# TensorE's order in the last attention: a written table of every score and transposed score in place of a string of letters

## The chip, the cores and the metric

The kernel runs on one core of a Trainium2 chip. The metric is the device time of one execution in microseconds (us), as the median of several runs; a profiled execution of the same program gives the trace. The engines are TensorE (PE; its weight loads are listed as PEld), VectorE (DVE), ScalarE (ACT), GpSimd (POOL) and SyncE (SP, which issues transfers).

## The reference, cut to what matters

A stream x of shape 2 x 512 x 512 (batch, position, width; float32) passes through eight blocks, each of the form x = x + block(layernorm(x)): four attentions and four feed-forward blocks. The change touches the last attention alone, a causal multi-head attention with 32 heads of 16:

```
qkv = hidden_states @ qkv_w + qkv_b
q, k, v = split into 32 heads of 16; rope on q and k
scores = einsum('bqhd,bkhd->bhqk', q, k) / 4, causal mask
probs  = softmax(scores)
ctx    = einsum('bhqk,bkhd->bqhd', probs, v)
return ctx @ out_w + out_b
```

## The kernel before, in words

The 32 heads are worked off as 8 quartets of four heads. A head's 16 features lie in a group of 32 partitions, so that the four heads of a quartet lie in the four row groups of TensorE, and matmuls of different heads g = 0 to 3 can run beside each other. Positions are cut into four tiles of 128. Everything is done once per batch, by `core(b, causal)`; a flag computed from the weights chooses the causal branch, which is the one that the trace shows.

For each quartet u there are these steps:

- `score(u, qt, g)` (L1572): the scores of query tile qt against keys 0 to 128 (qt + 1), so 128, 256, 384 or 512 columns, into a bank of PSUM. VectorE adds the mask and takes the row maximum (L1585), one column of the tile `nm[u % 2]`. 16 of them.
- `maxima(u)` (L1596): four transposes bring the maxima of the quartet into rows, and VectorE adds them to the queries (`qm`, L1601), so that the maximum comes off in the next product. It needs all 16 scores of the quartet.
- `transposed(u, kc, g)` (L1604): the transposed scores of key tile kc, 512, 384, 256 or 128 columns. ScalarE takes the exponential (L1621) into the tile `pt` of that key tile; after the fourth head GpSimd sets the upper triangle of the diagonal block to zero (L1625). 16 of them.
- `values(u)` (L1630): 16 matmuls over the four key tiles, in the order kc = 0 to 3, into one bank (L1636), copied to `raw` by ScalarE (L1644). Each key tile needs its mask of L1625.
- `divide(u)` (L1646): four transposes of `raw` (L1650), then a reciprocal and a product on VectorE (L1653, L1654).

Every step takes one of the eight banks of PSUM in rotation through `turn()`, so the step that stands eight places earlier must have been read (by VectorE for a score, by ScalarE for a transposed score) before a step can write.

TensorE's order is written by hand: within `tc.manual_schedule` (L1661) the steps stand on its queue as the Python code issues them. The other engines take the work in that order too. `run_ordered` (L389) issues eight scores in front, and then for each quartet walks the string `order`: S takes the next score from an iterator that goes through all quartets (tile by tile, heads in the order 0, 2, 1, 3), T the next transposed score of quartet u (key tile by key tile, heads 1, 3, 0, 2), M stands for the maxima of quartet u + 1, and | for the division of quartet u - 1. Values of quartet u follow at the end of the string. So scores run half a quartet to one and a half ahead of the transposed scores.

## Time and profile before

| what | us |
|---|---|
| median of 3 runs (lowest to highest) | 2110.02 (2104.93 to 2113.53) |
| the profiled execution | 2103.46 |
| its span, first to last instruction | 2101.4 |
| first score to first values, batch 0 (1785.11 to 1804.60) | 19.49 |
| five full periods from the first values to the sixth (1804.60 to 1855.21) | 50.61 |
| from the sixth values to the last division (1855.21 to 1876.40) | 21.19 |

The profiled execution has a time of its own, 2.1 us over its span. Times within the trace count from the span's start. A row of the windows view gives a stretch, its length, and each engine's busy time in it with the number of instructions; PEclk is the granted TensorE clock. A row of the timeline gives start, duration, engine, line, operation, output and inputs, and in brackets how long the engine had been idle and what released it. The last attention takes two stretches of the trace, one for each batch, from about 1785 and from about 1935 us.

### The profile page before, as it was taken

The page shows a single profiled execution, that of the slowest core. Times are in us where ns is not written, and L with a number is a line of the kernel's source. Part 1 is how long each engine was busy: PE and PEld are TensorE (multiplying, and loading weights), DVE is VectorE, ACT ScalarE, POOL GpSimd, SP SyncE. Part 2 cuts the span into 40 slices and gives each one's busy share as a digit, 9 for nine tenths or more (in the row PEclk, how much of TensorE's full clock was granted, in tenths as well). Part 3 has the DMA queues.
Part 4 walks back from the last instruction along what each step waited for, and adds up shares of the span by engine and source line. Part 5 has one row for each costly group of instructions (what it writes and reads, how often), then busy time and mean ns, then how long its engine had stood idle before and what let it go on. Part 6 is the DMA issues. An engine that isn't in the chain of part 4 may idle for free. (4 is left out here: it accounts for less than half of the span.)

```text
span 2101.4 us, 40138 instructions
## 1 busy us (share of the span) xinstructions
PE 2031.9 (97%) x15560; PEld 1147.1 (55%) x15560; DVE 1351.0 (64%) x3575; ACT 745.4 (35%) x2072; POOL 970.4 (46%) x1239
## 2 busy tenths in 40 slices
PE   9999999999999999999999989999999999999998
PEld 5444435666666566666665544545454454654654
DVE  7678766756566566666664557666666784855845
ACT  3555632222222222222222145444544411441531
POOL 1101016776555557566653246555555555115220
PEclk9999999999999999999999999999999999999999
DMA  3001012222222222222220321010101003002001
GB/s 100 16 21 41 1 66 76 72 76 71 91 71 71 91 71 76 71 91 76 73 77 26 117 61 54 22 51 25 50 22 52 2 6 70 2 2 41 2 2 40
DMA packets 70221, 107.43 MB, mean 51 GB/s; under 512 B 13699, under 2 KB 50691, under 8 KB 63237
## 3 DMA queue, kind: packets, MB, share of 16 engines
q1 hardware_dynamic: 69380, 103.71, 15.6%
q8 instruction: 126, 2.06, 0.4%
q10 hardware_dynamic: 640, 1.05, 0.3%
q14 instruction: 75, 0.61, 0.1%
HBM read 80.61 MB, written 2.10 MB: 39 GB/s over the span
## 5 line engine op out<-in xcount | busy, mean ns | idle before, releaser
L263 ACT ACTIVATE room<-room,nmax 128x128 f32<-128x128 f32 (+3 forms) x384 | 212.3, 555 | 484.2 <-DVE nmax L253 482.7
L274 POOL TENSOR_SCALAR room<-room,invs 128x128 f32<-128x128 f32 (+3 forms) x384 | 198.0, 537 | 142.1 <-DVE invs L271 142.1
L314 PE MATMUL sc<-turned,vals 32*128 32x128 f32 (+7 forms) x1034 | 186.2, 411 | 1.3 <-DVE turned L287 1.3
L314 PE MATMUL pj<-turned,vals 32*128 32x384 f32 (+7 forms) x708 | 184.9, 422 | 0.0
L210 POOL TENSOR_TENSOR rstd<-ve,mhalf 128x1 f32<-128x1 f32 x80 | 45.9, 577 | 246.0 <-DVE ve L208 240.2
L314 PE MATMUL tp<-turned,vals 32*128 32x256 f32 (+7 forms) x770 | 147.1, 420 | 2.5 <-DMA vals<-v 2.1
L242 PE MATMUL sc<-kT,q 128*32 128x256 f32 (+4 forms) x1528 | 134.0, 384 | 6.8 <-DVE invs L271 4.1
L287 DVE STREAM_TRANSPOSE turned<-room 128x1152 f32<-128x1152 f32 x80 | 109.1, 1363 | 42.4 <-POOL room L274 39.9
L314 PEld LDWEIGHTS sc<-turned,vals 32*128 32x128 f32 (+1 forms) x1034 | 119.3, 166 | 14.3 <-issue 4.2
L943 POOL TENSOR_TENSOR q<-q,cosq 128x512 f32<-128x512 f32 x60 | 89.5, 1491 | 59.9 <-DVE t L940 59.9
L162 PE MATMUL sc<-w,room 128*128 128x512 f32 (+1 forms) x256 | 112.1, 582 | 0.0
L314 PEld LDWEIGHTS pj<-turned,vals 32*128 32x128 f32 (+1 forms) x708 | 104.0, 169 | 4.0 <-issue 1.6
L314 PEld LDWEIGHTS tp<-turned,vals 32*128 32x128 f32 (+1 forms) x770 | 97.6, 169 | 10.8 <-issue 4.9
L162 PE MATMUL sc<-w,ctxT 128*128 128x512 f32 x224 | 101.5, 596 | 0.0
L218 DVE TENSOR_TENSOR x<-sc,x 128x512 f32<-128x512 f32 x79 | 54.2, 686 | 73.0 <-PE sc L162 70.3
L242 PE MATMUL tp<-kT,q 128*32 128x512 f32 (+4 forms) x984 | 91.7, 407 | 4.5 <-DVE invs L271 3.8
L274 POOL TENSOR_SCALAR probs<-probs,invs 128x128 f32<-128x128 f32 (+3 forms) x128 | 65.8, 535 | 65.0 <-DVE invs L271 61.2
L263 ACT ACTIVATE probs<-probs,nmax 128x128 f32<-128x128 f32 (+3 forms) x128 | 71.1, 556 | 65.5 <-DVE nmax L253 64.3
L253 DVE CUSTOM_DVE_ANT_0 room<-sc,mask 128x256 f32<-128x256 f32 (+3 forms) x149 | 70.7, 474 | 35.6 <-PE sc L242 34.1
L242 PE MATMUL pj<-kT,q 128*32 128x288 f32 (+3 forms) x968 | 89.6, 404 | 2.9 <-POOL q L1211 1.9
L944 POOL TENSOR_TENSOR q<-q,t 128x512 f32<-128x512 f32 x64 | 88.0, 1374 | 6.5 <-DVE q L943 2.5
L1208 POOL TENSOR_TENSOR t<-t,sinq 128x512 f32<-128x512 f32 x32 | 40.8, 1276 | 106.4 <-DVE invs L271 100.6
(621 smaller groups left out, 6232.9 us busy)
## 6 DMA issues: line engine op xcount, KB each, us to landing
w<-in_b_wq SPq DMA_DIRECT2D x16, 1024.0 KB, 4.9
w<-in_b_wo SPq DMA_DIRECT2D x16, 1024.0 KB, 5.2
vals<-v SPq DMA_DIRECT2D x256, 64.0 KB, 2.0
w<-in_m_wo SPq DMA_DIRECT2D x8, 1024.0 KB, 7.2
w<-in_b_wk SPq DMA_DIRECT2D x16, 256.0 KB, 2.5
w<-in_b_wupv SPq DMA_DIRECT2D x16, 256.0 KB, 2.5
w<-in_f_w SPq DMA_DIRECT2D x4, 1024.0 KB, 6.0
w<-in_m_wqn SPq DMA_DIRECT2D x8, 384.0 KB, 3.1
```

The source lines that it names most:

```text
L162: last = self.nc.tensor.matmul(out, lhsT, rhs, start=(i == 0), stop=(i == len(pairs) - 1))
L210: self.nc.gpsimd.tensor_tensor(r, ve, self.mhalf, ALU.pow)
L218: self.latest = self.nc.vector.tensor_tensor(self.x[t], ps, self.x[t], ALU.add).ins
L242: nc.tensor.matmul(ps[32 * i : 32 * i + 32, a - lo : b - lo], q[:, at : at + 32], keys[:, a:b], start=True, stop=True,)
L253: nc.vector.tensor_tensor_reduce(out=row, in0=ps[:, :kv], in1=self.mask_back[:, :kv] if qt % 2 else self.mask[:, S - kv :], op0=ALU.add, o ...
L263: nc.scalar.activation(row, row, AF.Exp, bias=nmax, scale=-1.0, accum_out=total[:, qt : qt + 1])
L274: self.nc.gpsimd.tensor_scalar(row, row, inv[:, qt : qt + 1], 1.0, ALU.mult, ALU.mult)
L287: self.nc.vector.transpose(out[:, :last], probs[:, :last])
L314: self.nc.tensor.matmul(out[:, :, :n], values(i, j), rhs, start=(j == blocks[0]), stop=(j == stop[i]),)
L943: mul.tensor_tensor(q, q, tables["cosq"], ALU.mult)
L944: nc.gpsimd.tensor_tensor(q, q, t2, ALU.add)
L1208: nc.gpsimd.tensor_tensor(t2, t2, sinq, ALU.mult)
```

## The change

`run_ordered` is replaced by `in_order`, and the string by a table. An entry such as `S21+1` is one step: the kind, the tile, the head, and how many quartets ahead of the round p it works (S score, T transposed, V values, D division, M maxima). `in_order` walks the table once for each p from -3 to 10 and leaves out entries whose quartet does not exist. So each round issues 16 scores, of quartets p + 1, p + 2 and p + 3, 14 transposed scores of quartet p and two of quartet p - 1, the values of p - 1, the division of p - 2 and the maxima of p + 1. The values stand fourth in the table, right behind the two last transposed scores of their quartet (T12-1, T31-1); division and maxima stand side by side. The steps themselves are not changed.

```diff
-    def run_ordered(n, lead, order, score, maxima, transposed, values, after):
-        scores = iter([(u, j, g) for u in range(n) for j in range(NT) for g in (0, 2, 1, 3)])
-        for i in range(lead):
-            score(*next(scores))
-        for u in range(-1, n):
-            left = [(j, g) for j in range(NT) for g in (1, 3, 0, 2)] if u >= 0 else []
-            for step in order:
...
-            if u >= 0:
-                values(u)
-        after(n - 1)
+    def in_order(n, order, do):
+        steps = [(s[0], int(s[1]), int(s[2]), int(s[3:])) if s != "|" else s for s in order.split()]
+        for p in range(-3, n + 3):
+            for step in steps:
+                if step == "|":
+                    if p > -3:
+                        do(p, step)
+                elif 0 <= p + step[3] < n:
+                    do(p + step[3], *step[:3])
...
-                order = "STTSTSSTSTTSTSTSTTTTS|TTSTMTSSSSSS"
-                k.run_ordered(8, 8, order, score, maxima, transposed, values, divide)
+                order = (
+                    "S21+1 T12-1 T31-1 V00-1 S01+2 T23+0 T32+0 S10+2 T11+0 S22+2 T03+0 S00+2 "
+                    "T02+0 T01+0 T10+0 S13+1 S12+2 T33+0 D00-2 M00+1 S02+3 T20+0 T21+0 S03+2 "
+                    "T22+0 S20+3 T13+0 S11+3 T30+0 S23+3 T00+0 S31+3 S32+2 S30+3 S33+3 "
+                )
+
+                def do(u, kind, *at):
+                    steps = dict(S=score, T=transposed)
+                    if kind in steps:
+                        steps[kind](u, *at)
+                    elif kind != "|":
+                        dict(M=maxima, V=values, D=divide)[kind](u)
+
+                k.in_order(8, order, do)
```

More of the change, by code (lines that the diff above doesn't have):

```diff
@@ L388, in run_ordered @@
     @staticmethod
-    def run_ordered(n, lead, order, score, maxima, transposed, values, after):
-        scores = iter([(u, j, g) for u in range(n) for j in range(NT) for g in (0, 2, 1, 3)])
-        for i in range(lead):
-            score(*next(scores))
-        for u in range(-1, n):
-            left = [(j, g) for j in range(NT) for g in (1, 3, 0, 2)] if u >= 0 else []
-            for step in order:
-                if step == "S":
-                    at = next(scores, None)
-                    if at:
-                        score(*at)
-                elif step == "T" and left:
-                    transposed(u, *left.pop(0))
-                elif step == "M" and u + 1 < n:
-                    maxima(u + 1)
-                elif step == "|" and u > 0:
-                    after(u - 1)
-            if u >= 0:
-                values(u)
-        after(n - 1)
+    def in_order(n, order, do):
[7 more added lines that the diff above has]
+                    do(p + step[3], *step[:3])
 def attn_latent_small(k, a):
```

## The prediction

> **What bounds the kernel now.** I read the page first, then the windows of this stage, then who the score reductions waited for, then the timeline of one quartet. The page:

> ```profile
> span 2101.4 us, 40138 instructions
> PE 2031.9 (97%) x15560; PEld 1147.1 (55%) x15560; DVE 1351.0 (64%) x3575; ACT 745.4 (35%) x2072; POOL 970.4 (46%) x1239
> ```

> TensorE (PE) is busy nearly everywhere, so whatever it is kept from in this stage lengthens the run. But four row groups of 32 work beside each other here, and "busy" means that at least one does. The windows tell more: ramp, full quartets and tail of the first batch, then one full quartet (from one block of values to the next).

> ```profile
> core 0: us, PE busy (x) PEld busy (x) DVE busy (x) ACT busy (x) POOL busy (x), PEclk, DMA share, GB/s
> 1785.11:1804.60 19.49, 16.75 (x121) 12.06 (x121) 17.70 (x74) 5.81 (x16) 2.05 (x4) 0.82 0.01 2
> 1804.60:1855.21 50.61, 50.54 (x520) 30.77 (x521) 42.71 (x178) 31.03 (x85) 12.60 (x21) 1.00 0.01 2
> 1855.21:1876.40 21.19, 21.10 (x200) 12.42 (x201) 9.41 (x34) 12.74 (x35) 5.72 (x9) 1.00 0.01 2
> 1834.97:1845.09 10.12, 10.11 (x104) 6.14 (x105) 8.54 (x38) 6.18 (x17) 2.54 (x5) 1.00 0.00 0
> ```

> A full quartet takes 10.12 us and holds 8.54 us of VectorE (DVE) work. The gap stands in one place:

> ```profile
> 1836.72 0.14 DVE L1585 DVE_READ_ACCUMULATOR2_ANT nm<- 128x1 f32 x1
> 1838.32 0.57 DVE L1585 CUSTOM_DVE_ANT_0 sc<-sc,mask 128x384 f32<-128x384 f32 x1 [1.45 <-PE pj L1575]
> 1834.97 1.06 PE L1636 MATMUL tp<-room,vs 128*32 128x512 f32 x8
> 1835.83 0.85 PE L1636 MATMUL tp<-pt,vs 128*32 128x384 f32 x8
> 1836.47 0.64 PE L1636 MATMUL tp<-room,vs 128*32 128x256 f32 x8
> 1836.90 0.43 PE L1636 MATMUL tp<-pt,vs 128*32 128x128 f32 x8
> 1837.26 0.58 PE L1575 MATMUL sc<-ks,qs 32*128 32x384 f32 x1
> ```

> For 2.29 us (1834.97 to 1837.26) TensorE does the values. VectorE has 1.9 us of scores in hand, then waits 1.45 us for the first new one; the rest of the period it runs without a gap, and TensorE waits for banks that it holds. So VectorE plus one hole sets 10.12 us. The streaming rate is read here too: eight passes over four column groups took 0.86 us for 512 columns, so 0.43 us a pass, 0.32, 0.21 and 0.11 for 384, 256 and 128. Each score and transposed score is two passes on its row group.

> The path of the transposed scores:

> ```profile
> 1829.81 0.62 ACT L1621 ACTIVATE room<-tp 128x512 f32<-128x512 f32 x1
> 1830.56 0.64 POOL L1625 TENSOR_SCALAR_AFFINE_SELECT room<-room 128x512 f32<-128x512 f32 x1 [5.09 <-ACT room L1621]
> 1873.13 0.64 POOL L1625 TENSOR_SCALAR_AFFINE_SELECT room<-room 128x512 f32<-128x512 f32 x1 [0.47 <-ACT room L1621]
> 1873.81 0.64 POOL L1625 TENSOR_SCALAR_AFFINE_SELECT pt<-pt 128x512 f32<-128x512 f32 x1
> ```

> The fourth exponential of a key tile ends at 1830.43, GpSimd's mask starts 0.13 us later and takes 0.64. The values of that tile need it. Before, key tile 0 is masked 4.4 us ahead of its values (1830.56 against 1834.97), so this costs nothing.

> **The change, part by part.** No instruction is added or removed: per batch 128 scores, 128 transposed, 8 maxima, values and divisions. ScalarE's, VectorE's and GpSimd's orders follow TensorE's; SP has nothing to do in the stage. The sums below are for one batch; there are two.

> *The ramp.* A reduction starts 0.245, 0.385, 0.515 or 0.65 us after the one before (1834.94, 1835.19, 1835.58; 1838.80 to 1839.31; 1791.26 to 1791.91), so 16 of them take 7.18 us. Before, the first maxima need 16 reductions: they start at 1793.49, 7.4 after the first reduction (1786.06). In the table 27 reductions stand in front (all of quartet 0, eleven of quartet 1): 12.2 us, so +5.0. From there to the second maxima VectorE has the maxima's wait 0.5, the sum 0.61, nine scores of 4.5 and six of 2.3: 8.0 us. It bounds this stretch, since the transposed scores stand behind banks that it must free. Then 4.6 us (next paragraph) to the first values: 12.7, against 1793.49 to 1804.60 = 11.1. The first values come 5.0 + 1.6 = 6.6 us later. ScalarE and TensorE idle meanwhile, and what is ahead must be given back later.

> *A full quartet.* I lay the table out on the four row groups from the first matmul after the maxima (0). T00 gets its bank from T21, whose exponential ends at 1.45; it starts at 1.5, its two passes 0.86 and the drain 0.16 end at 2.5, the exponential runs 2.6 to 3.2, the mask 3.33 to 3.97, and values may start at 4.05. Matmuls alone would be done at 3.45: T12, the last long one, waits for group 2, which S32 holds. So TensorE stands 0.6 us for GpSimd, a new wait, with everything else on its queue behind it. The mask of tile 1 (after T12: 4.18 to 4.82) then just meets its values at 4.91. Values to 6.34, then S01 is back at VectorE at 6.9. VectorE's last score in hand (S21) is done at 5.93: 1.0 us idle against 1.45. From S01 to division, maxima and next round takes 3.46 us on the busiest groups (ten 128-column steps of 0.213, plus 0.43 and 0.58 for the two blocks), with 0.3 us more of small VectorE gaps. Period 2.29 + 3.46 + 4.05 = 9.8 us; by VectorE 8.54 + 1.0 + 0.3 = 9.8. Only the four periods between the first and fifth values are full in the new table: 4 x (9.8 - 10.12) = -1.3 us.

> [...]

> *The tail.* Scores thin out in the last rounds, where ScalarE sets the pace: 16 exponentials 0.48, 0.37, 0.27 and 0.17 apart make 5.2 us, the copy of the raw values 0.6. The table puts the fourth transposed score of tile 0, then of 1 and of 3 at the end, so three masks follow the last exponentials. Laid out likewise, values 5 to 8 are 9.3, 9.1 and 8.7 us apart: 27.1, before 10.12 + 9.58 + 7.85 = 27.55. So -0.4. The penultimate division now stands behind the last values, under the copy of the raw tile (0.59 us): nothing.

> *The clock.* The row of the ramp shows a granted clock of 0.82: half clock from 1792.9 to 1799.7, after 2.3 us of waiting for the first maxima. [...] I take +0.6, near the trace's side.

> Sum of a batch: 6.6 - 1.3 - 0.4 + 0.6 = +5.5 us; two: +11. The profiled execution took 2103.46 us with a span of 2101.4; it stands 6.6 below the median of the three shown, 2110.02. +11 on either: 2114.5, or 2121 as median.

> **The rivals.**
> - *VectorE stays fed (not slower).* The table puts the four 512-column scores (2.6 us of reductions) just before the values, longer than the values' 2.29 us. If T00 ran 0.6 us earlier, its mask would be over before the matmuls are. Then the period nears VectorE's own 8.7 us: ramp +6, four periods -5.7, tail about 25 instead of 27.55, -2.5: -2.2 a batch, 2105.5. For it: 10.12 holds 1.45 of pure hole. Against it: even this ideal only just repays the ramp. Decided at mask 0 ending 3.4 us after the maxima; late by 0.6 us by my layout.
> - *TensorE collides.* The row groups in the table are uneven (ten steps on the longest group where an even share is 8.3; fourteen against 11.8), its queue is in order, and jitter adds up: a period of 10.4 instead of 9.8, and half a microsecond more in each tail round. +4 a batch, 2129. For it: S11 waits for the bank of the maxima and T30, T00 stand behind. Against: the passes of one group follow without a gap where banks are free (1838.01 to 1838.44, 0.43).
> - *The order is neutral*: the work that is ahead is all given back, 2110. Against: the tail can't use it, ScalarE paces it.

> **How the numbers follow.** Forecast case 0.57 (per batch +2 to +8.5: 0.36 of it slower by over 0.5%, 0.21 within); VectorE fed 0.20 (0.08 faster by over 0.5%, 0.12 within, since the ramp remains); collisions 0.20, slower; neutral 0.03, within. Sum: faster 0.08, same 0.36, slower 0.56; 0.5%, 10.5 us, is about what a measurement of this kernel can tell. Range: from the fed case's 2104 to 2138 (collisions and a median some us high). The forecast's own is 2113 to 2128.

> **What would show it.** Right: the first values some 26 us after the first score (before 19.5); L1636's counterpart waiting for POOL (before 1.2 us in all) by about 0.5 us a quartet; VectorE's hole near 1.0 us; values about 9.8 us apart in full rounds and 9 in the last three. Wrong: values 8.7 to 9.2 us apart with no wait for POOL (then not slower), or periods over 10.12.

## The result: 21.6 us slower, twice the forecast

| | median | lowest to highest |
|---|---|---|
| before, four runs | 2109.53 us | 2104.93 to 2113.53 |
| with the table, four runs | 2131.14 us | 2128.53 to 2134.32 |

The ratio is 1.011, with a 95% interval of 1.0092 to 1.0129. The direction is the one forecast, and the time lies in the range, but the change cost 21.6 us where 11 were forecast. The traces differ by more than the medians, since the profiled execution of the changed kernel (2134.32 us) is the slowest of its four and that of the kernel before (2103.46 us) is faster than all four of its own. The page of the changed kernel's profile:

```profile
span 2132.6 us, 40055 instructions
PE 2052.2 (96%) x15560; PEld 1167.1 (55%) x15560; DVE 1354.6 (64%) x3575; ACT 746.9 (35%) x2072; POOL 970.5 (46%) x1239
PEclk9999999999999999999999999999999998998999
```

The instructions of every engine are the same in number. What is new on the page is the last line: two slices of the 40 (from 1759 and from 1919 us) have a granted TensorE clock under nine tenths, where before none had, and they take in the two ramps of this attention. Over the whole run the mean granted clock went from 0.992 to 0.979.

The windows view of the changed kernel, in the order of the rows: the ramp of batch 0 (first score to first values), its next five periods, one full quartet, the ramp of batch 1, and the end of batch 0 from the seventh values to the first matmul of the output projection.

```profile
core 0: us, PE busy (x) PEld busy (x) DVE busy (x) ACT busy (x) POOL busy (x), PEclk, DMA share, GB/s
1790.44:1820.28 29.84, 27.68 (x150) 19.34 (x149) 25.71 (x104) 5.84 (x15) 1.28 (x2) 0.71 0.01 2
1820.28:1869.30 49.02, 46.03 (x504) 32.00 (x504) 41.78 (x167) 31.62 (x87) 12.55 (x21) 1.00 0.01 2
...
1840.06:1850.00 9.94, 9.42 (x104) 6.61 (x104) 8.71 (x38) 6.28 (x19) 2.50 (x4) 1.00 0.01 2
1952.29:1982.79 30.50, 28.50 (x148) 20.76 (x149) 25.44 (x105) 6.08 (x16) 2.65 (x4) 0.61 0.00 1
1878.27:1892.99 14.72, 13.58 (x121) 7.99 (x121) 2.05 (x6) 6.74 (x19) 3.57 (x6) 0.88 0.00 1
```

Before, the ramp took 19.49 us at a mean clock of 0.82; now it takes 29.84 at 0.71, and in batch 1 30.50 at 0.61. The periods did get shorter (49.02 for five instead of 50.61), and the last stretch has half clock too (0.88), where before the tail had 1.00. The clock in these traces is either full or half (in the first ramp 1.00 up to 1797.34, 0.50 to 1807.58, 1.00 to 1810.99, 0.50 to 1817.82, then 1.00), so the figure says how much of a stretch ran at half: 17.07 us of the first ramp and 23.89 of the second, where before it was 6.83 and 3.41. The forecast had read batch 0 of the kernel before alone. Its batch 1 is this row of the windows view:

```profile
1935.03:1953.16 18.13, 15.53 (x122) 11.45 (x123) 16.81 (x73) 5.98 (x17) 3.41 (x6) 0.91 0.01 1
```

So "before" wasn't 19.5 us twice, but 19.5 and 18.1.

From the first score to the output projection's first matmul the stage took 91.75 and 90.37 us before, and 102.54 and 103.46 after: +23.9 us. The two profiled spans differ by 31.2. Of the rest, 5.3 lie ahead of the first score (1785.11 against 1790.44), in code that the change doesn't touch, where these executions differ in half clock too (17.1 us of it before, 27.3 after); the variants below, with the same code there, start it anywhere from 1784.1 to 1793.9.

Behind the first maxima of the ramp VectorE now waits for TensorE, where the forecast had VectorE set the pace. Timeline of VectorE in the changed kernel, batch 0:

```profile
1813.50 0.43 DVE L1573 CUSTOM_DVE_ANT_0 pj<-pj,mask 128x256 f32<-128x256 f32 x1 [0.93 <-PE sc L1599]
...
1817.71 0.57 DVE L1573 CUSTOM_DVE_ANT_0 tp<-tp,mask 128x384 f32<-128x384 f32 x1 [0.84 <-PE tp L1563]
```

These two waits, 0.93 and 0.84 us, lie in the second of this ramp's two stretches of half clock (1797.34 to 1807.58 and 1810.99 to 1817.82). The reductions wait for transposed scores (L1599) and scores (L1563); a matmul of 512 columns takes 1.06 us there and 0.59 behind it. Waits of over 0.15 us for TensorE between first maxima and first values sum to 2.4 us in this ramp and to 3.1 in batch 1.

In a full quartet (timeline, from the matmul behind the maxima at 1845.87) the layout worked out for the forecast came nearly true:

```profile
1847.53 0.59 PE L1599 MATMUL tp<-qm,ks 32*128 32x512 f32 x1
...
1848.59 0.60 ACT L1609 ACTIVATE room<-tp 128x512 f32<-128x512 f32 x1 [0.49 <-PE sc L1563]
1849.31 0.64 POOL L1613 TENSOR_SCALAR_AFFINE_SELECT room<-room 128x512 f32<-128x512 f32 x1 [1.01 <-ACT room L1609]
1850.00 1.06 PE L1624 MATMUL tp<-room,vs 128*32 128x512 f32 x8 [0.52 <-POOL room L1613]
...
1852.84 0.30 DVE L1573 CUSTOM_DVE_ANT_0 sc<-sc,mask 128x128 f32<-128x128 f32 x1 [0.91 <-PE tp L1599]
```

T00 starts 1.66 us after the maxima (1.5 forecast), and the values stand for its mask until 4.13 us after them (4.05 forecast). VectorE's hole behind the values is 0.91 us (1.0 forecast, 1.45 before). What the matmuls of the values (PE alone, without the weight loads) waited for in the changed kernel, by the source view of their line (engine, tile, line: us in all, times):

```profile
  POOL room L1613: 11.3, 16
```

That is 0.52 us in a full quartet, as forecast (about 0.5), and up to 1.70 in the tail. Before, none of these matmuls waited for GpSimd; the 1.2 us that the forecast read were waits of weight loads.

### The profile page after: what moved, and what is told of

The parts are those of the page before. It is cut to its first block, busy times and chain, and to the rows that moved or that the text cites. A ratio compares the mean times of both kernels' runs of the same rounds, so it can differ in the third digit from the quotient of the medians.

```text
span 2132.6 us, 40055 instructions
## 1 busy us (share of the span) xinstructions
PE 2052.2 (96%) x15560; PEld 1167.1 (55%) x15560; DVE 1354.6 (64%) x3575; ACT 746.9 (35%) x2072; POOL 970.5 (46%) x1239
## 5 line engine op out<-in xcount | busy, mean ns | idle before, releaser
L1613 POOL TENSOR_SCALAR_AFFINE_SELECT room<-room 128x512 f32<-128x512 f32 x32 | 20.4, 637 | 162.9 <-ACT room L1609 162.9
```

Of the source, the lines that this page charges most:

```text
L1613: nc.gpsimd.affine_select(out=diag, in_=diag, compare_op=ALU.is_ge, fill=0.0, base=0, pattern=[[0, 4], [1, P]], channel_multiplier=-1,)
```

## The experiments

Every kernel below was timed beside the kernel before, whose median stands in brackets.

### 1. Shorter leads

`lead1` keeps the table's places and takes the scores from nearer quartets: one ahead up to the maxima, two behind them. So only quartet 0's scores stand in front of the first maxima.

```diff
-"S21+1 T12-1 T31-1 V00-1 S01+2 ... S10+2 ... S12+2 T33+0 D00-2 M00+1 S02+3 T20+0 T21+0 S03+2 T22+0 S20+3 ... S30+3 S33+3"
+"S21+1 T12-1 T31-1 V00-1 S01+1 ... S10+1 ... S12+1 T33+0 D00-2 M00+1 S02+2 T20+0 T21+0 S03+2 T22+0 S20+2 ... S30+2 S33+2"
```

> The new table with every score one quartet less ahead: the scores that stand before the maxima in a round lead by one quartet, those behind it by two; all else, and the order within a round, as in the new table. Theory 1 (the lead is what costs: 27 reductions instead of 16 before the first maxima, and the half clock that comes with the long wait): the first maxima come back to about 7.5 us after the first reduction, the first values to 20 to 23 us after the first score (29.8 and 30.5 in the new kernel, 19.5 and 18.1 before), periods stay at 9.95 us, and the time is 2110 to 2116. Rival (the order within the round costs, the lead is harmless): the time stays at 2126 or more.

Measured: 2129.77 us [2105.12], ratio 1.0115 (1.01 to 1.0129). The forecast of a gain is missed, though the step it was built on is there. The sum behind the first maxima starts 9.35 and 9.15 us after the first score, where the table has 14.36 and 14.11: the eleven scores in front of them cost the 5.0 us that the prediction gave them. But the ramp is only 3.5 and 4.4 us shorter (26.35 and 26.11), and the full periods went to 10.21 us. Here too the ramp ran at half clock for 17.07 us in each batch. Windows view of `lead1`, its two ramps:

```profile
1784.93:1811.28 26.35, 23.47 (x126) 16.08 (x125) 20.46 (x82) 5.74 (x15) 1.27 (x2) 0.68 0.01 2
1944.56:1970.67 26.11, 23.55 (x125) 15.80 (x125) 19.81 (x80) 5.91 (x15) 2.63 (x4) 0.67 0.00 1
```

VectorE's work in the first ramp fell from 25.71 to 20.46 us, yet the ramp fell by 3.5: VectorE isn't all that fills it.

### 2. The clock, by extra matmuls

If the half clock costs time, a run without it should be shorter. That added work takes it away was a guess, and these runs test both. The kernels with `warm` give TensorE more to do: they repeat the first scores of each batch, with the same operands and result, and transpose the identity in front of the first maxima into a tile that is then written anyway. The scheme, with the dose of `warm2_after`:

```diff
+            def times(u, qt, g):
+                issued.append((u, qt, g))
+                return 2 if len(issued) <= 45 else 1
...
-                nc.tensor.matmul(
+                for _ in range(times(u, qt, g)):
+                    nc.tensor.matmul(
...
+                for i in range(16 if u == 0 else 0):
+                    nc.tensor.transpose(tp[:, bass.ts(i % 4, P)], k.ident, k.ident)
```

The first try was the changed kernel with the first 39 scores done three times, and the kernel before with its first 24 (no transposes):

> The new kernel, in which the first 39 scores of a batch are each multiplied three times into the same bank with the same result, so that TensorE has more to do while it is paced by VectorE. Theory 1 (the part of the ramp that I had not forecast, about 4 us in the first batch and 5 in the second, is TensorE at half clock): no or much less half clock between the first score and the first values, the first values 25 to 27 us after the first score, the time lower by 6 to 9 us, 2122 to 2125. Rival (that part is waits for banks in the queue's order, and the clock is a bystander): half clock goes and the time stays at 2131, or grows by the added matmuls, up to 2138.

> The kernel before, in which the first 24 scores of a batch are each multiplied three times into the same bank with the same result. It tells what the half clock costs there (6.8 us of it in the first batch, 3.4 in the second, around the first maxima). Theory 1 (half clock in the ramp lengthens the time): lower by 1 to 4 us, 2106 to 2109. Rival (VectorE paces the ramp, the clock is a bystander): the same within 1 us, or longer by the added matmuls.

Measured: `warm_after` 2170.16 us [2105.12], ratio 1.0287 (1.0249 to 1.0325); `warm_before` 2121.02 [2105.12], ratio 1.0077. The gains looked for are missed: the dose was too high, and neither run tests what it was meant to test. (The six runs of `warm_after` spread from 2148.92 to 2195.45 us, and the trace is that of the first; what the others add isn't explained.) The half clock was gone from both ramps of `warm_after`, but they took 39.6 and 39.5 us, as the windows row of the first shows:

```profile
1786.11:1825.69 39.58, 39.08 (x305) 30.75 (x305) 27.90 (x104) 5.63 (x15) 1.28 (x2) 1.00 0.01 2
```

TensorE is busy for 39.08 of 39.58 us and VectorE for 27.90: three passes of each score on its row group made TensorE the pace. Hence a smaller dose, each score twice, on both kernels and on `lead1` (first 30 scores):

> The new kernel, with TensorE kept busier in the ramp at a dose that VectorE's pace leaves room for: each of the first 45 scores of a batch is multiplied twice into its bank with the same result, and 16 transposes of the identity are run into the bank of the first maxima before these, where TensorE stands for VectorE. (Three multiplications of each turned out to make TensorE itself the pace.) Theory 1 (the part of the ramp above my forecast is half clock): half clock in the ramp falls from 17 and 24 us to under 7, the first values come 25.5 to 27 us after the first score instead of 29.8 and 30.5, the time falls by 5 to 9 us, 2122 to 2126. Rival (the part is waits for banks): the first values stay at 29.5 to 31 us although the clock is up.

> The kernel before with the same dose: the first 24 scores of a batch twice, 16 transposes of the identity before the first maxima. Theory 1: little or no half clock in the ramp, the first values 17.5 to 18.5 us after the first score instead of 19.5 and 18.1, the time 1 to 3 us lower, 2102 to 2104. Rival (VectorE paces the ramp): the same first values, the same time.

> The shorter-lead table with the same dose over the first 30 scores. That table put the first maxima back to 9 us and still had its first values at 26 us, under 17 us of half clock. Theory 1 (half clock makes that ramp long): first values at 20.5 to 22.5 us, the time 2117 to 2122. Rival (the order behind the first maxima, nine scores ahead of the first transposed score and transposed scores behind banks that VectorE holds, makes it long at any clock): first values at 24 us or more, the time within 4 us of 2130.

| kernel | median [before] | ratio (95%) | ramps | half clock in them |
|---|---|---|---|---|
| warm2_after | 2126.62 [2106.03] | 1.010 (1.0078 to 1.0122) | 27.42, 27.37 | none |
| warm2_before | 2105.46 [2106.03] | 1.0000 (0.9988 to 1.0012) | 18.40, 18.10 | none |
| lead1_warm2 | 2122.82 [2106.03] | 1.0076 (1.0055 to 1.0097) | 22.71, 22.92 | none |

The first ramp of each, in this order, by the windows view:

```profile
1784.68:1812.10 27.42, 27.00 (x255) 21.87 (x254) 25.49 (x104) 5.73 (x15) 1.27 (x2) 1.00 0.01 3
```
```profile
1784.11:1802.51 18.40, 17.63 (x186) 13.70 (x186) 17.41 (x74) 5.93 (x16) 2.05 (x4) 1.00 0.01 3
```
```profile
1789.76:1812.47 22.71, 21.29 (x202) 16.16 (x202) 19.97 (x80) 5.74 (x15) 1.28 (x2) 1.00 0.01 3
```

With the dose in it (255 matmul records in the first ramp instead of 150), the changed kernel's ramp is 2.4 and 3.1 us shorter, and `lead1`'s 3.6 and 3.2. Both just miss what was expected of them (27.4 against 25.5 to 27; 22.7 and 22.9 against 20.5 to 22.5, and the times too). The median alone doesn't tell `warm2_after` from the changed kernel (1.010 against 1.011, with intervals that overlap); the ramps do. Added work can't shorten anything by itself, so the half clock cost at least that. The kernel before gained 1.1 us in its first ramp and nothing in its second (18.13 to 18.10), and its run stayed the same: there VectorE, 17.41 of 18.40 us, is the pace, as the prediction had said. What was true of the kernel before was carried over to a ramp where it isn't.

`warm2_after` still had half clock at the end of each batch. From the seventh values to the output projection batch 0 took 14.72 us at a mean clock of 0.88, like the changed kernel, with one stretch of 3.41 us; batch 1 had two stretches and took 16.41 us at 0.79. So two more kernels dosed the tail. `warm4_after` adds six transposes of the identity in front of the values of quartets 5 to 7; `warm3_after` has these and does the transposed scores of quartets 6 and 7 twice.

```diff
+                for i in range(6 if u >= 5 else 0):
+                    nc.tensor.transpose(acc[:, bass.ts(i % 4, P)], k.ident, k.ident)
```

> The new kernel with the dose in the ramp and, besides, in the tail: the transposed scores of the last two quartets are multiplied twice into their banks with the same result, and six transposes of the identity go into the bank of the values of the last three quartets before these, where TensorE stands for a mask. With the dose in the ramp alone, each batch still had 3.4 us of half clock at its end: the last period took 10.42 instead of 8.73 us, or the last values 4.0 instead of 2.4 us. Theory 1 (it is TensorE standing for the masks and ScalarE at the end that lowers the clock): no half clock up to the last values, last periods 8.7 to 9.1, last values 2.4 us, the time 2 to 5 us under that with the dose in the ramp alone, 2121 to 2125. Rival (the ends are disturbed by something else, or the added work costs what the clock gives): 2126 or more.

> The new kernel with the dose in the ramp and a lighter one in the tail: only the six transposes of the identity before the values of the last three quartets, where TensorE stands 0.5 to 0.9 us for a mask; no transposed score is doubled (doubling them made the last two periods 11.7 and 10.85 us, with no half clock left). Theory 1 (the ends of the new kernel pay for half clock that comes with standing for masks and exponentials): last periods 8.7 to 8.9, last values to the first matmul of the projection 4.4 to 5 us in both batches, together 3 to 5 us less than with the dose in the ramp alone, 2121 to 2124. Rival (0.65 us of transposes is too little to hold the clock in a period that ScalarE paces): one 3.4 us stretch of half clock per batch stays, 2126 to 2128.

`warm3_after`: 2129.28 us [2105.21], ratio 1.010. No half clock to the end of the attention, but the doubled transposed scores made the last two periods 11.7 and 10.85 us; overdosed again. `warm4_after`: 2121.16 us [2105.32], ratio 1.0079 (1.0064 to 1.0094), as expected, and with `lead1_warm2` and `mask_early_warm2` (below) the best of the table's variants. It has no half clock anywhere in the attention. Windows view, first ramp and tail of each batch:

```profile
1785.33:1812.76 27.43, 27.00 (x255) 21.88 (x254) 25.51 (x104) 5.73 (x15) 1.27 (x2) 1.00 0.01 2
1870.79:1884.32 13.53, 12.65 (x127) 7.79 (x127) 2.37 (x7) 6.88 (x19) 3.56 (x6) 1.00 0.00 1
...
2028.00:2041.53 13.53, 12.65 (x127) 7.79 (x127) 2.37 (x7) 6.88 (x19) 3.56 (x6) 1.00 0.00 1
```

The two batches are now alike (ramp 27.43 and 27.37, then 9.84, 9.94, 9.94, 9.94, 9.39, 8.98 and 8.73 us, and 4.80 to the output projection), and the tail takes 13.53 us instead of 14.72. From first score to output projection: 98.99 and 98.93 us, so 15.8 more than the kernel before where the changed kernel has 23.9 more. The dose isn't free: the first transposed score comes 18.27 us after the first score instead of 17.46, though the maxima are equally early, and the end takes 4.80 instead of 4.35. From these two differences I estimate it at 0.8 + 0.45 us a batch, 2.5 for both.

### 3. The mask's wait

`mask_early` exchanges T00 with T20 and T12 with S32 in the table, so that key tile 0's mask is done long before the values:

```diff
-"S21+1 T12-1 T31-1 V00-1 ... S02+3 T20+0 ... S23+3 T00+0 S31+3 S32+2 S30+3 S33+3"
+"S21+1 S32+1 T31-1 V00-1 ... S02+3 T00+0 ... S23+3 T20+0 S31+3 T12+0 S30+3 S33+3"
```

> The new table with two pairs exchanged: T00 with T20, and T12 with S32, so that the masks of key tiles 0 and 1 are due about 1 us earlier; the leads stay. Theory 1 (values stand about 0.6 us a quartet for the mask of tile 0): periods 9.3 to 9.5 instead of 9.95, the wait of the values for GpSimd under half of 37.5 us, the time lower by 4 to 8 us, 2123 to 2127. Rival (the row groups would hold the values back to the same point anyway): periods 9.8 to 10, 2131.

> The table with earlier masks and the same dose over the first 45 scores: the two repairs together. If both causes are right and independent: first values at 25 to 26.5 us, periods 9.85 as measured with earlier masks, the time 2117 to 2121. It stays over the kernel before in any case, since the 27 reductions before the first maxima remain.

Measured: `mask_early` 2127.31 us [2105.12], ratio 1.011 (1.0095 to 1.0125), no different from the changed kernel's 1.011; with the dose of `warm2_after`, 2122.31 [2106.03], ratio 1.0073 (1.0053 to 1.0093), its ramps 27.76 and 27.78, where 25 to 26.5 us and a time of 2117 to 2121 were expected. The periods are 9.85 us, 0.1 shorter, where 9.3 to 9.5 were expected, and 8.92, 8.57 and 8.46 in the tail. Waits of the values' matmuls (PE alone) in `mask_early`, and its full quartet in the windows view:

```profile
  POOL pt L1613: 4.3, 6
  POOL room L1613: 2.1, 4
```
```profile
1821.20:1831.05 9.85, 9.85 (x108) 7.19 (x106) 8.84 (x36) 6.35 (x17) 2.49 (x5) 1.00 0.01 3
```

All ten of these waits lie in the last three values of a batch. In a full quartet no matmul of the values waits for a mask any more, and TensorE is busy for the whole 9.85 us; yet the period moved by 0.1 of the 0.5 us. So the rival of this run held: without the mask the matmuls on the row groups reach the values at nearly the same time, 4.06 us behind the first matmul after the maxima (1826.98 to 1831.04) against 4.13. Whether their own work or the banks that they wait for hold them there stays open. (The 37.5 us in the expectation count weight loads too; with them it is 25.8 now, not the half that was expected.)

Two of the ramps show something else. Ramp of batch 1 in `mask_early`, then in `mask_early_warm2`:

```profile
1940.87:1967.82 26.95, 25.28 (x148) 18.60 (x148) 24.51 (x103) 6.25 (x16) 2.79 (x5) 0.75 0.00 1
```
```profile
1947.81:1975.58 27.77, 27.77 (x254) 22.13 (x254) 24.54 (x103) 6.24 (x16) 2.78 (x5) 1.00 0.02 4
```

The first has 13.7 us of half clock and no dose, the second a dose and no half clock, and the first is the shorter. Here half clock costs no more than the dose. All but 1.7 us of it lie ahead of the first transposed score, which comes 17.30 us after the first score; in batch 0 it is the same (10.2 us of half clock, all but 1.2 ahead, 27.25 against 27.76 us).

### 4. The lead in the old string

The remaining question was whether more scores in hand shorten a period at all. The kernel before with another lead than eight scores:

```diff
-                k.run_ordered(8, 8, order, score, maxima, transposed, values, divide)
+                k.run_ordered(8, 12, order, score, maxima, transposed, values, divide)
```

> The kernel before with 12 instead of 8 scores in front of the string, one number changed, so that the scores just before the values are of 256 and 384 columns instead of 128 and 256. Theory 1 (the period before is VectorE's work and the hole behind the values, which a larger score in hand fills, while the first maxima still wait for 16 reductions only): periods 9.2 to 9.6 us instead of 10.12, first values 0.5 to 2 us later, the time lower by 4 to 9 us, 2097 to 2102. Rival (TensorE's banks or row groups take over at once): periods 9.9 to 10.2, the time 2104 to 2110.

> The same with 16 scores in front: the six scores before the values have 384 and 512 columns, 3.6 us of reductions against the 2.3 us of the values. Theory 1: no hole at VectorE, periods 8.7 to 9.4, first values 2 to 3.5 us later, the time lower by 4 to 10 us against the kernel before, 2096 to 2102. Rival (as in the new table: more scores ahead lower TensorE's clock in the ramp, or TensorE sets the period): 2106 or more.

> The same with 6 in front, the least that leaves the sixteenth score of a quartet before its maxima in the string. Theory 1: period 9.8 to 10.0 us, unless the maxima must wait for the last score, which then stands two steps before them: 0.6 us of VectorE work more than is in hand there, so 10.4. Rival (a lead of eight is the best of this string): 10.3 us or more, 2109 or more.

> The kernel before with 7 instead of 8 scores in front of the string. With 12 and 16 in front the period grew from 10.12 to 10.73 and 11.40 us, against my expectation. Theory 1 (each score that is further ahead costs in the period, since it changes which score sizes meet the values, the division and the maxima): with 7 the period is about 10.0 us and the time 2 us lower, 2103. Rival (the string fits a lead of eight, any other is worse): 10.2 to 10.6 us, 2107 to 2112.

| lead | median [before] | ratio (95%) | full period, us | ramps, us |
|---|---|---|---|---|
| 6 | 2152.06 [2107.45] | 1.0195 (1.0176 to 1.0214) | 12.5 to 14.7 | 21.5, 21.4 |
| 7 | 2119.32 [2107.45] | 1.0048 (1.0034 to 1.0062) | 10.95 | 19.6, 19.2 |
| 8 (before) | | 1 | 10.12 | 19.5, 18.1 |
| 12 | 2113.82 [2105.21] | 1.0035 (1.0026 to 1.0045) | 10.73 | 20.2, 19.8 |
| 16 | 2131.99 [2105.21] | 1.0113 (1.009 to 1.0137) | 11.40 | 27.0, 23.1 |

The leads of 12 and 16 were expected to shorten the period, to 9.2 to 9.6 and 8.7 to 9.4 us, and missed. For those of 6 and 7 the rival held, a lead of eight is the best; 7 is longer than even that had it (10.2 to 10.6). At full clock the lead of 6 has 12.5 us, and its longer periods have 2.4 to 4.5 us of half clock in them. One quartet of the lead of 12 (windows view), and two waits of VectorE in it (timeline):

```profile
1830.80:1841.53 10.73, 10.48 (x106) 6.11 (x104) 8.92 (x36) 6.37 (x17) 2.51 (x5) 1.00 0.01 3
```
```profile
1834.34 0.70 DVE L1585 CUSTOM_DVE_ANT_0 av<-av,mask 128x512 f32<-128x512 f32 x1 [1.17 <-PE tp L1575]
...
1838.08 0.30 DVE L1585 CUSTOM_DVE_ANT_0 sc<-sc,mask 128x128 f32<-128x128 f32 x1 [0.30 <-PE pj L1611]
```

The hole behind the values shrank from 1.45 only to 1.17 us, and a wait of 0.30 us for transposed scores (L1611) is new. The eight banks go round in the order of issue, so another lead gives every step another predecessor to wait for; that this is the cause is my reading and isn't shown. Eight is the best of the five leads tried with this string. More scores in hand alone didn't help.

The lead of 16 also has the half clock in one order and one execution with no work added. Its two ramps in the windows view:

```profile
1785.49:1812.52 27.03, 26.94 (x138) 19.16 (x137) 21.50 (x92) 5.92 (x16) 2.54 (x4) 0.62 0.01 2
1951.54:1974.59 23.05, 22.49 (x136) 15.04 (x136) 20.30 (x89) 6.04 (x17) 3.91 (x6) 0.85 0.00 1
```

The first has 11.8 us of half clock behind its first transposed score, the second none there; it is 4.0 us longer, where the two batches of `warm2_before` differ by 0.3.

## Why the forecast was half of it

The stage by the prediction's own steps, in us per batch against the kernel before. The last column takes `warm4_after` less its dose, against `warm2_before`: both at full clock.

| step | forecast | batch 0 | batch 1 | at full clock |
|---|---|---|---|---|
| ramp | +6.6 | +10.3 | +12.4 | +8.2, +8.5 |
| four full periods | -1.3 | -0.8 | -0.6 | -0.8 |
| values 5 to 8 | -0.4 | +1.1 | -0.5 | -0.45 |
| from there to the output projection | 0 | +0.1 | +1.8 | +0.15 |
| clock | +0.6 | inside | inside | none |
| sum | +5.5 | +10.8 | +13.1 | +7.1, +7.3 |

No run settles what brings the half clock on. Both ramps of the changed kernel have TensorE busy for over nine tenths of the time (27.68 of 29.84 us and 28.50 of 30.50); the last section has more of what the traces show.

## What to carry to other kernels

A longer lead is paid at the start of each batch, in full, and is only worth it if the steady periods give it back; count them first (four here). When a change lengthens a stretch in which TensorE waits for another engine, cost that stretch at half clock too, and find part by part who sets the pace then: half clock was nearly free here where another engine did (0.3 us or less for 9 and 12 us of it), and an engine that sets it at full clock needn't do so at half. And read the figure that is subtracted in every batch, with the clock beside it: it may hold the same loss that is to be forecast.

## What the hardware showed unexpectedly

- A "busy" TensorE can stay at half clock. In batch 1 of the changed kernel it was busy for 94% of 23.89 us (seven times 3.41) at a clock of 0.50 throughout:

```profile
1957.77:1981.66 23.89, 22.57 (x114) 16.59 (x113) 19.49 (x83) 5.10 (x14) 0.64 (x1) 0.50 0.00 1
```

With the doubled scores it was busy for 27.00 of 27.42 us and had full clock (1.00). Busy means that at least one row group works: in the kernel before, four matmuls of 32 rows start between 1837.26 and 1837.28 and run for 0.58 to 0.69 us beside each other. In this stage the matmuls per us differ plainly: 5.9 a us in the 3.70 us ahead of that stretch, 11.4 in 3.41 us of `warm4_after`, and 10.5 in a full quartet of the changed kernel, all three at a clock of 1.00, and 4.8 in the stretch itself. But the count alone doesn't tell: the projection behind the stage has 10 matmuls of 128 rows and 512 columns in 3.41 us, 2.9 a us, at a clock of 1.00 (windows view, 1903.00 to 1906.41).
- Extra work can pay. 105 more matmul records made a ramp 2.4 us shorter, and 18 more transposes a batch made the end 1.2 us shorter (14.72 to 13.53).
- The dose is narrow. Scores done twice leave the ramp at 27.4 us, and three times at 39.6.
- No version tried beats the kernel before. Dosing that one gave 1.0000 (0.9988 to 1.0012), since half clock costs it next to nothing.
